# Layer 0 of a two-layer transformer kernel: two groups of transposes moved to a later stretch, and a PSUM copy with another priority

## The chip, the cores and the metric

The kernel runs on one core of one Trainium2 chip. The metric is the device time of one execution in microseconds; the kernel before takes 1139.03 us (median of 3 runs, 1138.77 to 1139.43).

TensorE (PE in the profile, PEld for its weight loads) multiplies matrices into PSUM. VectorE (DVE), ScalarE (ACT) and GpSimd (POOL) do the elementwise work, and SyncE (SP) issues most of the DMAs. Each engine runs its own instructions in order, and engines wait for each other by semaphores.

## What is computed

The input `x` is 4 sequences of 512 tokens with 256 features, all in float32. Four blocks follow each other, each added to its input after a layer norm without weights:

```
x = x + L0_attn(layernorm(x))   # 16 heads of 16, causal softmax, output projection w_out
x = x + L0_ffn(layernorm(x))    # per output feature: 8 router logits, the softmax's top 2
                                # weigh 8 expert outputs (expert_w); 2048 logits a token
x = x + L1_attn(layernorm(x))   # reads the array as (token, sequence): softmax over 4
                                # sequences, 16 query heads on 4 key heads of 128
x = x + L1_ffn(layernorm(x))    # gated MLP, 4-bit weights, 2048 inner features
```

The change touches the first block and the hand-over to the second.

## The kernel before

The tokens stay in SBUF (`xres`) as 16 groups of 128 tokens, in 4 blocks `j` of 4 groups; a block is a quarter of the causal order, for all 4 sequences.

**Layer 0 attention** runs over 44 batches `n`. A batch is a block of queries `j`, a sequence `s`, and 4, 2, 1 or 1 groups of 4 heads (for `j` = 0 to 3), so there are 4 batches in block 0, 8 in block 1 and 16 each in blocks 2 and 3. For each batch, `greatest` and `mask` make scores (L687, L700) whose maxima VectorE takes (L706); `shift` sends the maxima by DMA into an extra row of the queries. `powers` makes the scores again, transposed and shifted (L738), ScalarE takes the exponentials (L747), and GpSimd zeroes the masked triangle (L757). `mixed` multiplies them with the values (L774), and ScalarE copies the result out of PSUM (`avs`, L782). The score tiles share 5 PSUM banks (`ps_sc`), of which each of `greatest` and `powers` takes 4.

When the last heads of one `(j, s)` are mixed, `divided(j, s)` takes over. It transposes `avs` on TensorE (`av_T`, L792), divides by the sums on VectorE (`rden`, `oq`, L799 and L800), transposes the result back (`oq_T`, L809), and ScalarE copies it into `aT` (L812). After the fourth sequence, `aT` is multiplied with `w_out` (`o0`, L821) and added to `xres` (L831). Then `hidden_pieces(j)` normalises the new tokens (`norm_pieces`) and transposes them (`xT_ps`, L225) for the second block.

**Layer 0 FFN** is filler. `logit_pieces` and `result_pieces` each emit 64 products of 512 columns (`lg`, `eo`, both L249; 128 in all, each two matmuls), with VectorE work behind them (`weight_pieces`, `addition_pieces`) and ScalarE work (`lg` copies L312, `part` scalings L338, `spare` accumulations L430). What layer 0 leaves over goes on in layer 1 attention, where every `fill` gets a share of TensorE in proportion to the products left.

**Who orders the work.** The four compute engines run in the order in which the program emits, save for blocks under `tc.high_priority`. The order between the batches is planned by hand. Side work is written as generators (`Stream`) that yield `need(engine, cost, gap, cond)` before each step; `fill(PE=..., DVE=...)` opens one slot, counts `slot` up by one, and lets the streams go on while the budget of the engine that they ask for lasts. `gap` is the number of slots to pass after the stream's last step; `cond` must hold. The main loop does this for each batch:

```
with tc.high_priority(offset=AHEAD):      # AHEAD = 400
    greatest(n + 1); mask(n + 1); shift(n + 1)
fill(PE=..., DVE=2.6)                     # first stretch, an odd slot
with tc.high_priority(offset=AHEAD):
    mixed(n - 1); powers(n)
streams.insert(0, Stream(divided(...)))   # after the last heads of (j, s)
fill(PE=..., DVE=2.6)                     # second stretch, an even slot
```

`defer` puts ScalarE's accumulations off to the next slot. Those deferred in an odd slot come at the end of the next one, those deferred in an even slot at the start of the next one.

All side work that goes to PSUM shares the two banks of the pool `ps_dn`: `av_T`, `oq_T`, `xT_ps`, `lg`, `eo` and `o0`. A bank is free again when the engine that reads it is done.

When all 32 additions of the FFN are made, in head pass 10 of layer 1's 16, its weights' memory is given to the last block, and VectorE starts on the 4-bit weights (`dequant_pieces`).

Of the kernel before, what the change touches and what calls it, by code (L numbers as in the profile page):

```python
# [18 lines left out]
NS, NB = 4, 512  # L19
NT = 16  # L20
NC = 4
NBLK = 4
# [10 lines left out]
def tile_transformer(  # L33
# [18 lines left out]
    nc = tc.nc  # L52
# [56 lines left out]
    slot = 0  # L109

    def need(engine, cost, gap=0, cond=None):
        return engine, cost, gap, cond
# [54 lines left out]
    def norm_pieces(j, pool, small, out, deinterleave=False, cond=None):  # L167

        yield need("DVE", 1.0, cond=lambda: not normed and (cond is None or cond()))
        normed.append(j)  # L170
        st = small.tile([P, 4, 6], F32, tag="ln_st", name=f"ln_st{j}")
        mv = small.tile([P, 4, 2], F32, tag="ln_mv", name=f"ln_mv{j}")
        rs = small.tile([P, 4], F32, tag="ln_rs", name=f"ln_rs{j}")
        for t in range(4):
            if t == 2:
                yield need("DVE", 1.0)
            nc.vector.bn_stats(st[:, t, :], xres[:, 4 * j + t, :])
            nc.vector.bn_aggr(mv[:, t, :], st[:, t, :])
        yield need("DVE", 0.2)
        v = small.tile([P, 4], F32, tag="rs_v", name=f"rs_v{j}")  # L180
        nc.vector.tensor_scalar(v, mv[:, :, 1], EPS, None, ALU.add)  # L181
        nc.gpsimd.tensor_tensor(rs, v, minus_half, ALU.pow)  # L182
        xn = pool.tile([P, 4, HID], F32, tag="xn", name=f"xn{j}")
        for t in range(4):
            if t % 2 == 0:
                yield need("DVE", 0.9, not t)
            src, dst = xres[:, 4 * j + t, :], xn[:, t, :]
            if deinterleave:
                src = src.rearrange("p (k two) -> p two k", two=2)
                dst = dst.rearrange("p (two k) -> p two k", two=2)  # L190
            nc.vector.tensor_scalar(
                dst, src, mv[:, t, 0:1], rs[:, t : t + 1], ALU.subtract, ALU.mult
            )
        out.append(xn)
# [26 lines left out]
    def transposed(xn, hc, ps_pool, tag, name):  # L221

        ps = ps_pool.tile([P, 4, P], F32, tag=tag, name=name)
        for t in range(4):
            nc.tensor.transpose(ps[:, t, :], xn[:, t, hc * P : (hc + 1) * P], ident)  # L225
        return ps
# [52 lines left out]
    def hidden_pieces(b):  # L279

        out = []
        done = (4 * b - 5, 1)
        last = b == NBLK - 1
        yield from norm_pieces(b, b1, b2, out, cond=lambda: b < 2 or done in halves)
        xT = b2.tile([P, 2, 512], F32, tag="xT", name=f"xT{b}")
        for hc in range(2):
            yield need("PE", 0.5, 0 if hc else 1 + last)
            ps = transposed(out[0], hc, ps_dn, "dn", f"xT_ps{b}_{hc}")
            ps = ps.rearrange("p t q -> p (t q)")
            if hc:  # L290
                nc.scalar.activation(xT[:, hc, :], ps, AF.Identity, bias=last_16)
            else:
                nc.scalar.copy(xT[:, hc, :], ps)
        normed.clear()
        xTs[b] = xT
# [168 lines left out]
    with ExitStack() as l0:  # L464
# [202 lines left out]
        AHEAD = 400  # L667
# [116 lines left out]
        aTs = {}  # L784

        def divided(j, s):

            yield need("PE", 0.5, 1)
            avs = avs_of.pop((j, s))
            ps = ps_dn.tile([P, NH0, 32], F32, tag="dn", name=f"av_T{j}_{s}")  # L790
            for g in range(4):
                nc.tensor.transpose(  # L792
                    ps[:, 4 * g : 4 * g + 4].rearrange("p h d -> p (h d)"), avs[:, g], ident
                )

            rden = a2.tile([P, NH0], F32, tag="rden", name=f"rden_{j}_{s}")
            oq = a1.tile([P, NH0, 16], F32, tag="oq", name=f"oq_{j}_{s}")
            left["DVE"] -= 0.7
            nc.vector.reciprocal(rden, ps[:, :, 16])  # L799
            nc.vector.tensor_tensor(  # L800
                oq, ps[:, :, 0:16], rden.unsqueeze(2).to_broadcast([P, NH0, 16]), ALU.mult
            )

            yield need("PE", 0.3, 1, cond=lambda: slot % 2)
            if not s:
                aTs[j] = a1.tile([P, 2, 16, NS, 8], F32, tag="aT", name=f"aT{j}")
            ps = ps_dn.tile([P, 2, P], F32, tag="dn", name=f"oq_T{j}_{s}")
            for k in range(2):
                nc.tensor.transpose(  # L809
                    ps[:, k], oq[:, 8 * k : 8 * k + 8].rearrange("p h d -> p (h d)"), ident  # L810
                )
            nc.scalar.copy(aTs[j][:, :, :, s, :], ps.rearrange("p k (g b) -> p k g b", b=8))  # L812
            if s < NS - 1:
                return

            for t in (0, 2):
                yield need("PE", 1.75, 1 if j or not t else 0)
                ps = ps_dn.tile([P, 2, HID], F32, tag="dn", name=f"o0_{j}_{t}")
                for i in range(2):
                    for k in range(2):  # L820
                        nc.tensor.matmul(  # L821
                            ps[:, i],
                            lhsT=aTs[j][:, k, 4 * (t + i) : 4 * (t + i) + 4].rearrange(
                                "p g s b -> p (g s b)"
                            ),
                            rhs=wo[:, k, :], start=k == 0, stop=k == 1,
                        )
                if j:
                    yield need("DVE", 0.7, 1)
                both = xres[:, 4 * j + t : 4 * j + t + 2, :]  # L830
                nc.vector.tensor_tensor(both, both, ps, ALU.add)  # L831
            fold_at = streams.index(fold) if fold in streams else len(streams) - 5
            streams.insert(fold_at if j else 0, Stream(hidden_pieces(j)))


        ps = ps_mm.tile([P, 4, P], F32, tag="mm", name="idle")
        for i in range(5):
            nc.tensor.matmul(
                ps, lhsT=ident, rhs=ident.unsqueeze(1).to_broadcast([P, 4, P]),
# [46 lines left out]
        for n in range(NBT):  # L886
            j, s, gs = batches[n]
# [20 lines left out]
            if n and batches[n - 1][2][-1] == 3:  # L908
                streams.insert(0, Stream(divided(*batches[n - 1][:2])))
# [13 lines left out]
        mixed(NBT - 1)  # L923
        streams.insert(0, Stream(norm_pieces(0, b1, b2, normed_first)))
        last = Stream(divided(*batches[NBT - 1][:2]))
        streams.insert(0, last)
        while last.next is not None:
# [49 lines left out]
    with ExitStack() as l1:  # L977
# [249 lines left out]
        for p in range(-1, NP):  # L1227
            j, kv = divmod(p, NKV)
# [59 lines left out]
    with ExitStack() as f1:  # L1288
# [186 lines left out]
        f, k = firsts  # L1475
# [3 lines left out]
        for i in range(NBLK * NJ):  # L1479
            j, jj = divmod(i, NJ)  # L1480
# [12 lines left out]
            e, g = eg[:, 0], eg[:, 1]  # L1493
# [147 lines left out]
```

## Time and profile before

| | |
|---|---|
| median of 3 runs | 1139.03 us |
| profiled execution, own time | 1140.53 us |
| profiled execution, span | 1138.8 us |
| granted TensorE clock, mean | 0.999 |
| busy PE, PEld | 1109.8 us, 711.7 us |
| busy DVE, ACT, POOL | 842.3 us, 509.5 us, 247.2 us |
| `oq_T` L809, matmuls | 32, 6.3 us |
| `xT_ps` L225, matmuls | 64, 11.6 us (layer 0's and layer 1's) |
| `aT` L812, copies | 16, 5.9 us |

Layer 0 attention ends and layer 1 begins at about 385 us of the span, and the last block begins at about 820 us. The profile is one execution, and its span leaves out what lies before the first and after the last instruction. Ends of matmuls are modelled, so a busy TensorE can contain waits; they are seen in the distance from one block's start to the next.

### The profile page before, as it was taken

How to read it: one execution, taken by the hardware profiler on the slowest of the kernel's cores; microseconds unless marked ns; L12 is line 12 of the kernel's file. 1: busy time of each engine (PE TensorE's matmuls, PEld its weight loads, DVE VectorE, ACT ScalarE, POOL GpSimd, SP SyncE). 2: the span in 40 equal slices, each digit the busy share in tenths (PEclk: the TensorE clock that was granted, in tenths of full speed). 3: DMA queues.
4: the chain of work that ended last, by engine and by line, in shares of the span. 5: the costliest groups of instructions: out<-in, count | busy, mean ns of one | idle time of the engine just before them, and what ended most of it. 6: DMA issues, size and time to landing. Idle time of an engine off the chain costs nothing.

```text
span 1138.8 us, 19760 instructions
## 1 busy us (share of the span) xinstructions
PE 1109.8 (97%) x7430; PEld 711.7 (62%) x7430; DVE 842.3 (74%) x1856; ACT 509.5 (45%) x1190; POOL 247.2 (22%) x319
## 2 busy tenths in 40 slices
PE   9999999999999999999999999999999999999998
PEld 5666555555555445555555556556787788888885
DVE  6675988999999962867873695577479877778665
ACT  1445545665556543444444353243324444444442
POOL 8322222221111000000000000000064444353433
PEclk9999999999999999999999999999999999999999
DMA  4450010000000500000000002242002002002000
GB/s 133 110 134 5 17 25 2 2 1 3 2 2 2 184 2 1 1 1 1 1 1 1 1 2 37 66 110 68 18 1 54 22 19 75 1 19 75 18 2 19
DMA packets 32287, 35.13 MB, mean 31 GB/s; under 512 B 6024, under 2 KB 23176, under 8 KB 32192
## 3 DMA queue, kind: packets, MB, share of 16 engines
q1 hardware_dynamic: 31376, 32.69, 11.0%
q10 hardware_dynamic: 816, 1.18, 0.4%
q8 instruction: 59, 0.97, 0.3%
q14 instruction: 36, 0.29, 0.1%
HBM read 23.17 MB, written 6.29 MB: 26 GB/s over the span
## 4 chain that ended last, share of the span: by engine, by line
PE 67%; DVE 23%; ACT 4%; issue 3%; POOL 1%; DMA 1%; SPq 1%; DVEq 0%; POOLq 0%; ACTq 0%
PE qk_ps L1037 10%; PE lg_ps L249 8%; PE o L1128 8%; PE eg L963 7%; PE eo L249 7%; PE gu_first L963 5%; DVE mx L706 3%; PE yx L1344 3%; PE s L738 3%; PE s L687 3%; PE av L774 2%; PE yy L1344 2%; DVE it L1420 2%; DVE th L1419 2%; PE qk_ps L555 2%
## 5 line engine op out<-in xcount | busy, mean ns | idle before, releaser
L1037 PE MATMUL qk_ps<-xT,wqkv 128*128 128x512 f32 x320 | 148.7, 599 | 3.5 <-ACT v L1023 1.7
L249 PE MATMUL lg_ps<-rw,xT 128*128 128x512 f32 x256 | 122.5, 601 | 1.6 <-ACT aT L812 0.4
L249 PE MATMUL eo<-ew,xT 128*128 128x512 f32 x256 | 121.5, 600 | 1.1 <-ACT lg L312 0.5
L706 DVE TENSOR_REDUCE mx<-s 128x1 f32<-128x384 f32 (+3 forms) x176 | 100.5, 633 | 26.8 <-PE s L700 26.8
L1128 PE MATMUL o<-wpj,oT 128*128 128x256 f32 x512 | 119.1, 382 | 0.0
L757 POOL TENSOR_SCALAR_AFFINE_SELECT pt<-pt 128x256 f32<-128x256 f32 (+2 forms) x88 | 62.5, 715 | 243.3 <-ACT pt L747 242.5
L1128 PEld LDWEIGHTS o<-wpj,oT 128*128 128x128 f32 x512 | 96.0, 190 | 27.0 <-issue 13.5
L1037 PEld LDWEIGHTS qk_ps<-xT,wqkv 128*128 128x128 f32 x320 | 59.1, 190 | 73.2 <-issue 58.4
L747 ACT ACTIVATE pt<-s 128x512 f32<-128x512 f32 (+1 forms) x176 | 84.0, 563 | 37.6 <-PE s L738 37.6
L182 POOL TENSOR_TENSOR ln_rs<-rs_v,minus_half 128x4 f32<-128x4 f32 x12 | 13.6, 1135 | 366.0 <-DVE rs_v L181 366.0
L338 ACT ACTIVATE part<-eo,c 128x256 f32<-128x256 f32 x128 | 53.6, 472 | 84.0 <-PE eo L249 72.7
L1531 ACT COPY gu_first<-eg 128x512 f32<-128x512 f32 x28 | 16.0, 570 | 134.2 <-PE eg L963 129.9
L249 PEld LDWEIGHTS eo<-ew,xT 128*128 128x128 f32 x256 | 46.2, 190 | 46.3 <-issue 38.5
L249 PEld LDWEIGHTS lg_ps<-rw,xT 128*128 128x128 f32 x256 | 46.1, 190 | 46.3 <-issue 37.5
L1322 POOL TENSOR_TENSOR it<-it 128x512 f32<-128x512 f32 x30 | 38.2, 1273 | 146.6 <-PE gu_first L963 66.9
L312 ACT COPY lg<-lg_ps 128x512 f32<-128x512 f32 x64 | 37.6, 588 | 71.8 <-PE lg_ps L249 71.8
L1041 ACT COPY qT<-qk_ps 128x512 f32<-128x512 f32 x64 | 37.5, 586 | 64.7 <-PE qk_ps L1037 64.7
L1344 PE MATMUL yx<-it,wd 128*128 128x256 f32 x240 | 66.2, 379 | 0.0
L738 PE MATMUL s<-qk 32*128 32x128 f32 x1280 | 56.6, 287 | 0.7
L687 PE MATMUL s<-qk 32*128 32x128 f32 (+3 forms) x512 | 56.7, 465 | 0.4
L438 DVE SCALAR_TENSOR_TENSOR junk<-lg,w 128x256 bf16<-128x256 f32 x128 | 54.9, 429 | 0.0
L365 DVE TENSOR_TENSOR part<-part 128x512 f32<-128x512 f32 x32 | 22.4, 700 | 43.9 <-ACT part L338 43.9
(305 smaller groups left out, 2202.5 us busy)
## 6 DMA issues: line engine op xcount, KB each, us to landing
qk<-stage SPq DMA_DIRECT2D x56, 64.0 KB
wqkv<-in_w_qkv SPq DMA_DIRECT2D x8, 320.0 KB
rw<-in_router_w SPq DMA_DIRECT2D x8, 256.0 KB
ew<-in_expert_w SPq DMA_DIRECT2D x8, 256.0 KB
qk<-mT SPq DMA_DIRECT2D x128, 0.5 KB
wpj<-in_w_proj SPq DMA_DIRECT2D x1, 2048.0 KB
dq_sgu<-in_gate_up_s SPq DMA_DIRECT2D x64, 32.0 KB
xres<-in_x SPq DMA_DIRECT2D x3, 512.0 KB
```

Of the source, the lines that this page charges most:

```text
L249: nc.tensor.matmul(ps, lhsT=xT[:, hc, (g % 4) * P : (g % 4 + 1) * P], rhs=w[:, hc, 2 * pair : 2 * pair + 2, :].rearrange("p e o -> p (e o) ...
L338: nc.scalar.mul(part[:, e % 4], ps[:, i], c[:, e : e + 1])
L438: stt(junk, d[:, e], 0.0, w1, ALU.is_gt, ALU.mult, accum_out=c1[:, e : e + 1])
L687: nc.tensor.matmul(tiles[h][:, b * nk : (b + 1) * nk].rearrange("p (c k) -> p c k", k=P), lhsT=queries(j, g)[r, s], rhs=qk[r, g, : j + 1, ...
L706: nc.vector.tensor_reduce(maxes[:, :nb, h], ps[:, : nb * nk].rearrange("p (b k) -> p b k", b=nb), AX.X, ALU.max,)
L738: nc.tensor.matmul(tiles[h][:, at : at + P], lhsT=qk[r, g, c, s, :], rhs=queries(j, g)[r, s], start=True, stop=True,)
L747: nc.scalar.activation(pt[:, i, : nb * nk], tiles[2 * pair + i][:, : nb * nk], AF.Exp, scale=0.25)
L757: nc.gpsimd.affine_select(out=last, in_=last, compare_op=ALU.is_ge, fill=0.0, base=0, pattern=pattern, channel_multiplier=-1,)
L963: nc.tensor.matmul(ps[:, w], lhsT=lhs(w), rhs=rhs, start=start and not i and not w, stop=i == len(terms) - 1 and w == 1, skip_group_check= ...
L1037: nc.tensor.matmul(ps, lhsT=wqkv[:, hc, kv, h, :], rhs=xT[:, hc, :], start=hc == 0, stop=hc == 1,)
L1128: nc.tensor.matmul(ys[t // 2][:, t % 2], lhsT=state["o"][:, h, t * P : (t + 1) * P], rhs=wpj[:, HPK * kv + h, :], start=kv == 0 and h == 0 ...
L1344: nc.tensor.matmul(ps, lhsT=lhs(jj), rhs=its[8 * j + jj][:, plane], start=start and not n, stop=n == 1, skip_group_check=not start,)
```

## The change

The step that transposes the divided output (`oq_T`) waited for an odd slot, the first stretch; it now waits for an even one, the second stretch, except for the last batch (block 3, sequence 3), where any slot will do. The transposes of normalised tokens in `hidden_pieces` were asked for one slot after the norm's last step, in the last block two; now it is two in every block. The copy of `oq_T` into `aT` is emitted under the same high priority as the batches' own work.

```diff
@@ hidden_pieces
         done = (4 * b - 5, 1)
-        last = b == NBLK - 1
         yield from norm_pieces(b, b1, b2, out, cond=lambda: b < 2 or done in halves)
         xT = b2.tile([P, 2, 512], F32, tag="xT", name=f"xT{b}")
         for hc in range(2):
-            yield need("PE", 0.5, 0 if hc else 1 + last)
+            yield need("PE", 0.5, 0 if hc else 2)
@@ divided
+            last_batch = j == NBLK - 1 and s == NS - 1
             yield need("PE", 0.5, 1)
...
-            yield need("PE", 0.3, 1, cond=lambda: slot % 2)
+            yield need("PE", 0.3, 1, cond=lambda: last_batch or not slot % 2)
...
-            nc.scalar.copy(aTs[j][:, :, :, s, :], ps.rearrange("p k (g b) -> p k g b", b=8))
+            with tc.high_priority(offset=AHEAD):
+                nc.scalar.copy(aTs[j][:, :, :, s, :], ps.rearrange("p k (g b) -> p k g b", b=8))
```

## The prediction

> **What bounds the kernel now.** I read the page's busy shares and slices first, then the busy times by stage, then TensorE's timeline through layer 0.
>
> ```profile
> PE 1109.8 (97%) x7430; PEld 711.7 (62%) x7430; DVE 842.3 (74%) x1856; ACT 509.5 (45%) x1190; POOL 247.2 (22%) x319
> ...
> DVE  6675988999999962867873695577479877778665
> ```
>
> TensorE is the bound of the whole span. In slices 6 to 14, which are layer 0's late batches, VectorE is nearly as full. The same by stage (us, then busy us of PE, PEld, DVE, ACT, POOL, granted clock, DMA share, GB/s):
>
> ```profile
> 150.00:395.00 245.00, 238.51 (x2360) 127.63 (x2359) 228.01 (x548) 140.29 (x382) 43.66 (x63) 0.99 0.06 19
> 395.00:700.00 305.00, 301.64 (x1442) 165.95 (x1441) 200.26 (x514) 135.31 (x351) 3.34 (x3) 1.00 0.02 6
> 166.00:171.00 5.00, 4.80 (x58) 3.40 (x58) 4.93 (x13) 1.91 (x4) 0.14 (x1) 0.66 0.01 3
> ```
>
> From 150 to 395 us VectorE is busy 228.0 of 245 us and TensorE 238.5: two engines at their limit. In layer 1 (second row) VectorE has 105 us to spare and TensorE 3. PE's busy time contains waits inside its blocks, so stalls must be read from the starts of blocks. TensorE's timeline (start us, us, block, idle and releaser):
>
> ```profile
> 165.17 0.40 PE L700 MATMUL s<-later,ident_h 128*128 128x128 bf16 x4
> 166.20 0.44 PE L809 MATMUL oq_T<-ident,oq 128*128 128x128 f32 x2 [0.63 <-DVE oq L800]
> 166.61 2.21 PE L225 MATMUL xT_ps<-ident,xn 128*128 128x128 f32 x8
> 168.75 1.51 PE L774 MATMUL av<-pt,va 128*32 128x128 f32 x24
> ...
> 182.51 0.86 PE L774 MATMUL av<-pt,va 128*32 128x128 f32 x24
> ...
> 195.14 0.40 PE L700 MATMUL s<-later,ident_h 128*128 128x128 bf16 x4
> 196.58 0.41 PE L809 MATMUL oq_T<-ident,oq 128*128 128x128 f32 x2 [1.04 <-DVE oq L800]
> ```
>
> Each transpose asked for in the first stretch waits for VectorE's division, which is queued behind filler work. At 166 us three such waits meet, the clock drops to half for about 3 us (0.66 in the row 166:171), and the next block takes 1.51 us where its like takes 0.86. Last, ScalarE's queue in front of the last transposed copy, and the output product that waits for it:
>
> ```profile
> 373.29 0.42 ACT L430 ACTIVATE spare<-owing__4754 128x256 bf16<-128x256 f32 x1 [2.95 <-DVE owing__4754 L423]
> ...
> 373.70 0.35 ACT L812 COPY aT<-oq_T 128x256 f32<-128x256 f32 x1
> ...
> 374.11 1.99 PE L821 MATMUL o<-wo,aT 128*128 128x256 f32 x8 [1.73 <-ACT aT L812]
> ```
>
> The copy had its input at about 369.9 us, but stood behind an accumulation that waited 2.95 us for VectorE.
>
> **The change, part by part.** No instruction is added or removed; every term is a shift in the engines' order. I call the fill after the maxima of batch n stretch nA and the one after its powers nB.
>
> 1. The transposes of the divided output go from A to B. With normal spacing from mask to next block of 0.23 us, the mask at 165.17 is followed after 1.03, the one at 195.14 after 1.44, and the one at 224.35 after 0.53 (224.88). Excess 0.79 + 1.21 + 0.29 = 2.3 us. In B they stand behind the mixed values and the powers, 1.8 us later; the division is done by then. Gain 2.3 us.
>
> 2. Transposes of normalised tokens, one slot later for blocks 0 to 2. Eight took 2.49 us from 88.28 to the next block at 90.77, and 2.14 us from 166.61 to 168.75; at about 0.11 us each they need 0.88. Of the excess of 1.6 + 1.25 us, I leave some 0.5 for ScalarE's copy, which the logits need at once in either order. Gain 2.3 us, and the 0.65 us of the half-clock block (1.51 against 0.86).
>
> 3. The copy on ScalarE. In the built order it stands straight behind the four exponentials of its batch in all 15 ordinary cases, and in the last case ahead of the accumulations that blocked it. It stands in the same places with the priority taken out, since the accumulations of a B stretch are put out at its end anyway: the word "priority" buys nothing by itself, and the move to B does. Gain: TensorE's idle 1.73 us at 374.11 and 0.40 us before logits at about 286. Holding a dn bank until the exponentials end (four of 0.56 us) is covered by the one product of 1.75 us that follows.
>
> 4. The last batch. Its transposes now stand straight behind those of its mixed output, with no product between (before: one, 1.72 us). They wait for reciprocal and product, 0.24 + 0.42 us and two hand-overs: a loss of about 1.0 us.
>
> 5. Filler thins out. Counting products (two matmuls of 512 columns, 4 x 0.43 = 1.72 us) by stretch in the built orders, layer 0 holds 63 before and 59 after; all 128 are done by head pass 11 of layer 1 in both, and TensorE's order is the same from pass 12. Four products, 6.9 us, leave layer 0 and return in layer 1: no net cost if TensorE is the bound in both. But they leave uneven stretches. Without a product (or nearly) are 19A, 41A and 42A before; 07A, 17A, 18A, 20A, 22A, 26A, 29A, 39A and 40A after. What an empty stretch costs, TensorE shows:
>
> ```profile
> 214.24 0.95 PE L738 MATMUL s<-qk 32*128 32x128 f32 x24
> 215.01 2.47 PE L687 MATMUL s<-qk 32*128 32x384 f32 x8
> ...
> 339.99 2.85 PE L738 MATMUL s<-qk 32*128 32x128 f32 x32
> ...
> 347.70 1.95 PE L738 MATMUL s<-qk 32*128 32x128 f32 x32
> ```
>
> An empty A lengthens the powers behind it: 1.95 us where 1.17 is normal (0.8), and in block 2 1.50 for 0.95 (0.55). That is 2.15 us before (0.55 + 2 x 0.8) and 5 x 0.55 + 4 x 0.8 = 5.95 after. An empty B lets the next scores wait for the exponentials: 2.47 for 0.93, 1.54 us; with only the first transposes in it, 0.75 to 1.16. Stretches 06B, 16B, 19B, 23B, 27B and 36B make 7.2 us before; 06B, 20B, 24B, 28B, 35B and the missing product of 43B (about 1.9) make 6.5 after. Loss 3.8 - 0.7 = 3.1 us.
>
> Sum: 2.3 + 2.3 + 0.65 + 2.1 = 7.35 gained, 1.0 + 3.1 lost: about -3.2 us, taken as -3.0. Bounds of the unknown: an empty A may cost nothing, where VectorE would have made TensorE wait anyway, or as much as the worst late-maxima row (2.85 us, 1.68 over normal). I take the middle since the rows at 183 and 348 us are empty A's themselves.
>
> 6. Layer 1: the division of labour moves some 40 VectorE instructions there, into its 105 us of room. The dequantisation ends one step later; its last product (1.23 us) then falls behind the last softmax instead of ahead of it, into an 8 us wait of VectorE for the residual. SP's transposing loads for the last stage come after the third weight load, some 80 us before use. GpSimd's roots move with the norms; it is 22% busy. Zero.
>
> The profile's span is 1138.8 us and its own time 1140.53, 1.5 us above the median of 1139.03. With -3.0 the span would be 1135.8, the profile's time 1137.5, and the median 1136.0.
>
> A rule against the change: the Trainium skill, "TensorE: Matmul & The Clock Gate", section "HAM oscillation", asks that TensorE have no idle gap over about 3.4 us, or its clock halves. The row 166:171 halved with no idle of more than 0.63 us between blocks, so the measurement is stricter than the page. By the page the thinned stretches cost nothing; by the row, one more thin spell (06B with 07A, or 16B to 18A) could cost the same 0.65 us or a little more.
>
> **The rivals.** (a) VectorE sets the pace of layer 0. For: 93% busy there, and 4.9 us less of its work, by instruction means, stands before the last maxima. Then TensorE's saved waits are absorbed: -4.9 to the last maxima, -1.7 for the product missing in the tail, -1.7 + 1.0 for items 3 and 4 there, +6.9 in layer 1: -0.4 us, 1138.6. Against: TensorE's own blocks of a full batch (7.2 us) also fill the period.
>
> (b) Slower: the powers behind the empty A's wait for late maxima. Six more such stretches at 1.68 us instead of 0.55 to 0.8 cost 10.1 us in place of 3.8, and -3.0 becomes +3.3: 1142.3. It decides from about 1.1 us for each empty A. For: two batches' filler is now asked for in one B, and VectorE's segment before the maxima of batch 20, 23, 28 and 37 sums to 8.1 to 8.8 us. Against: equally long segments stand before, at other batches.
>
> (c) The priority reorders nothing: already in item 3, no change to the sum.
>
> **How the numbers follow.** Forecast (-3.0, between -2.4 and -6.0) 0.46; (a) 0.24; (b) 0.30. About 0.2%, 2.3 us, is what a measurement of this kernel can tell from no change, so these are the chances of faster, same and slower. The range runs from 1133.0, the forecast with most of the 3.8 us of empty A's free, to 1143.0, a little beyond (b).
>
> **What would show it.** Right: oq_T without idle before it except once at the end; o<-wo,aT without wait for the copy; clock 1.00 around 160 to 180 us; layer 1 starting some 8 to 10 us sooner and taking some 7 us longer. Wrong: powers (L738) of 2 us and more at 17, 20, 22, 26 and 39; a second half-clock spell; or a layer 1 that stalls where the late products fall.

## The result: slower, and outside the predicted range

| | before | after |
|---|---|---|
| median | 1139.23 us (4 runs) | 1154.82 us (4 runs, 1153.45 to 1154.91) |
| ratio | | 1.0127 [1.0112, 1.0142] |
| profiled execution: span, own time | 1138.8, 1140.53 us | 1153.1, 1154.79 us |
| layer 1's first head pass | 393.5 us | 400.7 us |
| last block's first product | 815.6 us | 830.0 us |

Forecast was 1136.0 us, with a range of 1133 to 1143. Layer 0 became 7.2 us longer, where some 8 to 10 us less were expected. Layer 1 became 7.2 us longer (429.3 against 422.1), close to the predicted 6.9 (but see point 6). The last block is unchanged (323.1 against 323.2). Some executions of single kernels ran at a much lower granted clock; they are left out of every ratio, and the profiles of e4 and e11, which show such executions, are not compared.

The page of the changed kernel, its busy shares and VectorE's 40 slices:

```profile
PE 1117.1 (97%) x7430; PEld 717.6 (62%) x7430; DVE 841.7 (73%) x1856; ACT 508.5 (44%) x1190; POOL 243.3 (21%) x319
...
DVE  7666758999999756676974485677568877778665
```

The same instructions, and TensorE "busy" 7.3 us longer: its blocks hold more waiting inside. VectorE has a hole in slices 5 and 6 (7 and 5 tenths), where it was at 9 and 8 before. By stage (us, then busy us of PE, PEld, DVE, ACT, POOL, granted clock, DMA share, GB/s), the changed kernel:

```profile
150.00:395.00 245.00, 234.55 (x2392) 128.25 (x2391) 218.53 (x525) 134.46 (x368) 39.06 (x63) 0.99 0.04 11
400.70:830.00 429.30, 424.41 (x2174) 241.92 (x2172) 285.43 (x685) 184.79 (x436) 6.43 (x5) 1.00 0.10 24
150.00:200.00 50.00, 46.12 (x449) 25.86 (x447) 34.73 (x87) 22.15 (x61) 7.50 (x13) 0.93 0.08 12
```

and the last stretch in the kernel before:

```profile
150.00:200.00 50.00, 47.98 (x480) 26.17 (x481) 46.34 (x112) 26.39 (x73) 11.77 (x15) 0.97 0.04 7
```

Between 150 and 200 us both engines that were at their limit are idle for longer, VectorE by 11.6 us. I measured each block of TensorE from its start to the next one's and took off the usual distance of its kind. What is left between 30 and 400 us is 25.8 us before and 40.9 after, 15.1 more. By releaser, the powers' wait for VectorE's maxima goes from 7.7 to 16.2 us (a batch's powers need score banks that the maxima of the next batch still hold; I call this wait late maxima); the rest are waits that hardly stood in the profile before. TensorE's timeline of the changed kernel shows all kinds (start us, us, block, idle and releaser):

```profile
61.25 0.38 PE L809 MATMUL oq_T<-ident,oq 128*128 128x128 f32 x2
62.30 1.12 PE L554 MATMUL qk_ps<-xT,wp 128*128 128x512 f32 x2 [0.66 <-DVE oq L800]
...
96.01 0.60 PE L225 MATMUL xT_ps<-ident,xn 128*128 128x128 f32 x4
98.08 0.66 PE L225 MATMUL xT_ps<-ident,xn 128*128 128x128 f32 x4 [1.47 <-ACT aT L813]
...
152.58 3.70 PE L249 MATMUL eo<-ew,xT 128*128 128x512 f32 x8
...
157.07 0.40 PE L699 MATMUL s<-later,ident_h 128*128 128x128 bf16 x4
160.16 3.48 PE L822 MATMUL o<-wo,aT 128*128 128x256 f32 x8 [2.69 <-ACT part L337]
...
176.08 2.40 PE L737 MATMUL s<-qk 32*128 32x128 f32 x24
178.41 0.44 PE L809 MATMUL oq_T<-ident,oq 128*128 128x128 f32 x2
178.69 0.60 PE L225 MATMUL xT_ps<-ident,xn 128*128 128x128 f32 x4
180.33 1.11 PE L225 MATMUL xT_ps<-ident,xn 128*128 128x128 f32 x4 [1.04 <-ACT aT L813]
...
349.05 2.26 PE L737 MATMUL s<-qk 32*128 32x128 f32 x32
351.23 0.66 PE L792 MATMUL av_T<-ident,avs 128*128 128x128 f32 x4
```

- **Late maxima.** The powers of batch 17 take 2.33 us (176.08 to 178.41) where 24 such matmuls take 0.88; those of batch 40 2.18 where 32 take 1.10. Behind the nine empty stretches A that the prediction named the excess is 1.88, 1.45, 0.67, 1.80, 1.59, 0.67, 1.03, 0.85 and 1.08 (07 to 40): 11.0 us.
- **Held banks.** At 98.08 and 180.33 xT_ps waits for the copy aT, which stands behind four exponentials. At 62.30 (and twice more in block 0) the projections wait for the division, since av_T and oq_T stand in one stretch and hold both dn banks.
- **A staging transfer.** Two products `eo0_0` and `eo0_1` stand in one stretch (152.58, 8 matmuls). Their scaling on ScalarE waits 4.90 us:

```profile
159.27 1.57 ACT L337 ACTIVATE part<-eo,c 128x256 f32<-128x256 f32 x4 [4.90 <-DMA qk<-stage]
```

The tile `part` reuses the buffer of `stage3_1`, whose DMAs still read it. Before the change the two products stood in different stretches, and a wait of 3.77 us at this place let one bank free, so that TensorE did not stop for it. Now both dn banks are held, o0_1_2 waits 2.69 us for one, until 160.16.

- **Half-clock spells.** Within that last wait, at 159.8 us, TensorE's clock falls to half for 3.4 us, and so it does at 180.3 us (within the second wait of xT_ps) and at 439.7 us, in layer 1. The profile before has one such spell, at 167.0 us. A spell costs at most half its length, so the two more are worth up to 3.4 us (an estimate from the rows).

```profile
159.80:163.20 3.40, 3.04 (x7) 2.50 (x8) 1.54 (x3) 1.03 (x3) 0.00 (x0) 0.50 0.01 1
180.30:183.60 3.30, 3.27 (x7) 1.92 (x8) 1.70 (x3) 1.15 (x2) 1.22 (x2) 0.50 0.00 0
439.70:443.10 3.40, 3.40 (x5) 1.35 (x4) 3.37 (x16) 0.57 (x1) 0.00 (x0) 0.50 0.00 0
```

### The profile page after: what moved, and what is told of

It reads as the page before. It is cut to its first block, busy times and chain, and to the rows that moved or that the text cites. A ratio compares the mean times of both kernels' runs of the same rounds, so it can differ in the third digit from the quotient of the medians.

```text
span 1153.1 us, 19741 instructions
## 1 busy us (share of the span) xinstructions
PE 1117.1 (97%) x7430; PEld 717.6 (62%) x7430; DVE 841.7 (73%) x1856; ACT 508.5 (44%) x1190; POOL 243.3 (21%) x319
## 4 chain that ended last, share of the span: by engine, by line
PE 71%; DVE 21%; ACT 3%; issue 2%; POOL 1%; DMA 1%; SPq 1%; DVEq 0%; POOLq 0%; ACTq 0%
PE qk_ps L1038 10%; PE o L1129 8%; PE eo L249 8%; PE lg_ps L249 8%; PE eg L964 7%; PE gu_first L964 5%; PE s L737 3%; PE yx L1345 3%; PE s L686 3%; DVE mx L705 3%; PE v_ps L1020 2%; PE av L773 2%; PE yy L1345 2%; DVE it L1421 2%; DVE th L1420 2%
## 5 line engine op out<-in xcount | busy, mean ns | idle before, releaser
L756 POOL TENSOR_SCALAR_AFFINE_SELECT pt<-pt 128x256 f32<-128x256 f32 (+2 forms) x88 | 58.5, 670 | 259.8 <-ACT pt L746 259.7
L737 PE MATMUL s<-qk 32*128 32x128 f32 x1280 | 62.0, 287 | 2.3 <-DVE mx L705 1.2
L737 PEld LDWEIGHTS s<-qk 32*128 32x128 f32 x1280 | 48.5, 185 | 16.6 <-issue 8.5
```

Source lines behind the costliest of these rows:

```text
L737: nc.tensor.matmul(tiles[h][:, at : at + P], lhsT=qk[r, g, c, s, :], rhs=queries(j, g)[r, s], start=True, stop=True,)
L756: nc.gpsimd.affine_select(out=last, in_=last, compare_op=ALU.is_ge, fill=0.0, base=0, pattern=pattern, channel_multiplier=-1,)
```

## The experiments

Theory T: the two moves together make the filler uneven, and waits of several kinds, late maxima above all, come up behind it. Rivals: the PSUM bank held behind the exponentials, the later tokens, the staging transfer. Medians of "before" differ between sets (1139.2 to 1140.6 us), so runs are compared by ratio; the last column is (ratio - 1) x 1139.

| | edit | ratio [95%] | us |
|---|---|---|---|
| | the change | 1.0127 [1.0112, 1.0142] | +14.5 |
| e1 | oq_T to B, priority | 1.0002 [0.9992, 1.0011] | +0.2 |
| e2 | later tokens only | 0.9969 [0.9959, 0.9979] | -3.5 |
| e6 | the change, block 0's tokens as before | 0.9999 [0.9990, 1.0009] | -0.1 |
| e8 | later tokens in blocks 1 and 2, priority | 1.0000 [0.9991, 1.0010] | 0.0 |
| e3 | the change, oq_T in another pool | 1.0104 [1.0079, 1.0130] | +11.8 |
| e4 | the change, staging tile elsewhere | 1.0093 [1.0076, 1.0110] | +10.6 |
| e9 | e3 and e4 | 1.0061 [1.0038, 1.0084] | +6.9 |
| e10 | the change, one product a stretch | 1.0041 [1.0026, 1.0055] | +4.7 |
| e13 | e10 and e3 | 1.0037 [1.0025, 1.0050] | +4.2 |
| e5 | the change, oq_T booked at 0.0 | 1.0035 [1.0024, 1.0045] | +4.0 |
| e14 | the change, oq_T booked at 0.5 | 1.0071 [1.0053, 1.0088] | +8.1 |
| e7 | before, six stretches A emptied | 1.0114 [1.0094, 1.0134] | +13.0 |
| e11 | e2 and priority | 0.9954 [0.9941, 0.9967] | -5.2 |
| e12 | e11 and larger budgets | 1.0007 [0.9996, 1.0019] | +0.8 |

### Each move alone: e1, e2, e6, e8

```diff
 e1, against the change
-            yield need("PE", 0.5, 0 if hc else 2)
+            yield need("PE", 0.5, 0 if hc else 1 + last)
 e2, against before
-            yield need("PE", 0.5, 0 if hc else 1 + last)
+            yield need("PE", 0.5, 0 if hc else 2)
 e6, against the change
-            yield need("PE", 0.5, 0 if hc else 2)
+            yield need("PE", 0.5, 0 if hc else (1, 2, 2, 2)[b])
 e8, against before (and the copy under high priority)
-            yield need("PE", 0.5, 0 if hc else 1 + last)
+            yield need("PE", 0.5, 0 if hc else (1, 2, 2, 2)[b])
```

e1: 

> Only the transposes of the divided output move to the second stretch, with the copy's priority; the normalised tokens' transposes stay where they were before. In the built order layer 0 then holds as many filler products as before (before 59 in the stretches between batches, changed kernel 56), and six stretches A that the changed kernel leaves empty (07, 17, 18, 20, 22, 26) are filled. Theory T (the loss comes from the thinned stretches, which only the two moves together make, and from the wait of the part scaling at 155 us): close to before, 1137 to 1141 us, powers late by under 10 us in all where the changed kernel has 16. Rival B (the move to B itself costs, since the PSUM bank of oq_T is held behind the exponentials): 1147 us or more, with waits of xT_ps, o and lg for the copy aT. Rival G (the gap of two slots costs): before minus 2 to 3, 1136.

e2: 

> Only the transposes of normalised tokens move one slot later; the transposes of the divided output stay in the first stretch and the copy keeps its old priority. Layer 0 again holds 59 products, with 33A and 41A newly or still empty and 17A, 19A, 42A filled. Theory T: 1136 to 1140 us, a little below before, for the waits of xT_ps for the normalised tokens (1.2 us) and the half-clock block are gone. Rival B: the same. Rival G (a later start of the logits is what costs): 1147 us or more.

e6: 

> The changed kernel with the tokens' transposes of block 0 alone asked for one slot later instead of two; blocks 1 and 2 keep two. In the built order this alone brings back 59 products and fills 07A, 14A, 17A, 18A, 20A, 22A, 26A, 29A, 39A and 40A. Theory T': the whole loss hangs on block 0's first transposes being a slot later in a kernel whose oq_T is in B, which delays the first logits and thins every stretch behind: 1138 to 1141 us, VectorE busy 46 us or more of the 50 from 150 us on (changed kernel 34.7). Rival: the later slots of blocks 1 and 2 carry part of it: 1145 to 1150 us.

e8: 

> The kernel before, with the tokens' transposes of blocks 1 and 2 alone one slot later and the copy's priority; oq_T stays in the first stretch. The two waits of xT_ps for the normalised tokens and the half-clock spell go (3 us in the prediction's rows, less the 1 to 1.5 us of logits that then wait for the copy xT), and the last copy no longer stands behind an accumulation (up to 1.7 us): 1135 to 1138 us. Rival (the gain of the kernel with only the later slots, 3.5 us, came from block 0): 1139.

Neither move costs anything alone: the first changes nothing (+0.2), the second gains 3.5 us. Together they lose 14.5. And the loss hangs on one slot: with block 0's transposes back in their old slot (e6) the changed kernel is as fast as before. In its stage row VectorE's hole is gone and the clock is full; e6:

```profile
150.00:200.00 50.00, 48.38 (x529) 26.28 (x531) 47.74 (x114) 28.31 (x77) 9.17 (x15) 1.00 0.07 11
```

The block around 96 us shows the slot. In e6 block 0's tokens are transposed in 07A, ahead of the powers, and oq_T stands alone with a product behind them; in the changed kernel all of it stood in 07B, behind powers that had no cover, in the banks that oq_T held. e6:

```profile
94.45 1.98 PE L249 MATMUL lg_ps<-rw,xT 128*128 128x512 f32 x4 [0.24 <-ACT xT L292]
96.36 1.08 PE L773 MATMUL av<-pt,va 128*32 128x128 f32 x32
97.37 1.17 PE L737 MATMUL s<-qk 32*128 32x128 f32 x32
98.47 0.44 PE L809 MATMUL oq_T<-ident,oq 128*128 128x128 f32 x2
98.75 1.88 PE L249 MATMUL lg_ps<-rw,xT 128*128 128x512 f32 x4
```

e8 answered a side question: the later slots of blocks 1 and 2, which carried most of the prediction's 2.3 + 0.65 us, gain nothing. Nor did the priority: the last output product still waits 1.74 us for the copy in e8's timeline (before: 1.73). So most of what e2 gains must come from block 0's slot too, which with oq_T in A fills 17A, 19A and 42A. In e2's profile layer 1 is shorter (418.6 us for the same 63 products, before 422.1) and layer 0 longer; but this is the slowest of e2's nine executions (1138.86 us, the fastest 1134.82), so where the gain lies is not settled.

### The waits one by one: e3, e4, e9

```diff
 e3, against the change
-            ps = ps_dn.tile([P, 2, P], F32, tag="dn", name=f"oq_T{j}_{s}")
+            ps = ps_mm.tile([P, 4, P], F32, tag="mm", name=f"oq_T{j}_{s}")[:, :2]
 e4, against the change
-                        [P, 2, 512], F32, tag="hi4" if j == 2 else "part", name=f"stage{j}_1"
+                        [P, 2, 512], F32, tag="hi4" if j == 2 else "xn", name=f"stage{j}_1"
```

e3: 

> The changed kernel with the PSUM tile of oq_T in the pool of the projections instead of the two dn banks; the order of all engines is that of the changed kernel. Theory T: the waits for the copy aT in front of xT_ps (1.5 us) and of block 0's projections for the division (1.5 + 0.8 us) go, the late powers stay at about 16 us: 1151 to 1153 us. Rival B (banks held behind the exponentials are the main cost): 1144 us or less. If the projections' own pool becomes the wait instead: 1154 to 1156.

e4: 

> The changed kernel with the last staging tile of the positions' columns (stage3_1) in the buffers of the normalised tokens instead of those of part, so that the first scaling part0_0 does not wait for the staging DMAs; the order of the compute engines is that of the changed kernel. Theory T counts 3 to 5 us for this wait (4.9 us of ScalarE at 159 us, o0_1_2 2.7 us late, the half-clock block after it): 1149 to 1152 us, and a clock of 1.00 from 150 to 200 us. Rival T' (late maxima behind thin stretches alone): 1154 us, the next wait takes its place within two batches. Rival S (the staging wait is the whole of it): 1145 us or less.

e9: 

> The changed kernel with both of the earlier edits: oq_T in the projections' PSUM pool, and the last staging tile in the buffers of the normalised tokens; the order of the compute engines stays that of the changed kernel. One at a time they gave 4.5 and 3.4 us. If they are separate waits the sum is 8 us: 1147 us, with the late powers still at 16 us in the trace: then the other 7 us are the thin stretches' (theory T). If one wait takes the other's place: 1149 to 1151. If the two are all of the loss: 1141 or less.

By ratio e3 gives back 2.7 us, e4 3.9, both together 7.6. (The expectation of e9 has larger figures for each, taken from medians of two sets.) The interval of e3 overlaps that of the change, so its 2.7 us alone is not clear of noise; e4 and e9 are. The figures fit two separate waits that are together about half of the loss (by the interval of e9, some 5 to 10 us). The late maxima are untouched by either: 16.6 us in e3 and 15.3 in e9, the changed kernel 16.2.

### The spread of the filler: e10, e5, e14, e13

```diff
 e10, against the change: products (lg and eo) wait for the next stretch if this one has one
+                    room() and g // 4 in xTs and (0, pair) in folded ...
+                    and room() and h in weights and weights[h][1] < slot ...
 e5 (0.0) and e14 (0.5), against the change
-            yield need("PE", 0.3, 1, cond=lambda: last_batch or not slot % 2)
+            yield need("PE", 0.0, 1, cond=lambda: last_batch or not slot % 2)
```

e10: 

> The changed kernel with one more condition: no stretch of layer 0's batches takes a second filler product. Both moves stay, block 0's late chain too, and layer 0 keeps the changed kernel's 56 products; only their spread is evener: from batch 16 on the stretches A without a product are 16, 29, 35, 39 instead of 17, 18, 20, 22, 26, 29, 39, 40. Theory T (a price for each empty stretch A, about 1.2 us in the changed kernel and 2 us in the kernel made for it): 1147 to 1150 us. Rival (the late chain itself costs, wherever the products stand): 1153 to 1156.

e5: 

> The changed kernel with one number changed: the step that emits oq_T is booked at 0.0 of the slot's TensorE budget instead of 0.3. Both moves and the priority stay, but layer 0 gets its 59 products back and the empty stretches A from batch 16 on go from 17, 18, 20, 22, 26, 29, 39, 40 to 17, 18, 33, 42; with it block 0 is as before the change up to batch 12. Theory T (uneven filler and late maxima behind it): 1138 to 1143 us, late powers of 8 to 11 us. Rival H (both moves together delay the FFN's chain, whatever the filler does): 1150 us or more.

e14: 

> The changed kernel with oq_T booked at 0.5 instead of 0.3. In layer 0 three products fewer than the changed kernel (53); from batch 16 on the empty first stretches are 25, 27, 38, 39, 41 (changed kernel: eight), the empty second ones 16, 17, 18, 20, 24, 28, 29, 35, 40 (changed kernel: 20, 24, 28, 35, 43). If only empty first stretches cost: 1147 to 1149 us. If empty second ones cost as well, 1 to 1.5 us each as the scores wait for the exponentials: 1151 to 1156 us, with the waits of scores for exponentials at 10 us or more in place of 6.

e13: 

> The changed kernel with at most one filler product in a stretch of layer 0 and with oq_T in the projections' PSUM pool. Alone they gave 9.2 and 4.5 us. If the two causes are separate the sum is 13 to 14 us: 1140 to 1142 us, which with the staging wait (gone with the spread) is the whole loss. If they share their gain: 1143 to 1145 us, and a third cause is open.

Both moves stay in all four, and block 0's tokens are late in all. e10 spreads the products and gives back 9.8 us, more than expected: late maxima fall to 12.4 us, scores waiting for exponentials from 6.2 to 3.9, and the staging wait no longer reaches TensorE, since the two `eo` stand apart. e5 gives back 10.5 us by another way, one number of the booking (1143.91 us, just above its range). So the spread is the main cause, and not a late chain in itself.

The built order shows how the number acts. In block 2 a stretch B has 2.2: 2.2 - 0.3 - 1.85 leaves 0.05, and what is above zero lets a second product in; the account is then at -1.80, and the next A's 1.8 leaves nothing. 21B and 25B hold oq_T and two products, 22A and 26A are empty. Booked at 0.0, 0.3 us is left for the A, which gets its product.

e14 landed where T's first branch put it (1147.44 us), but nearly with the second branch's sign: scores wait 9.6 us for exponentials instead of 6.2, and late maxima still take 13.3. An empty B is paid for as well, here with 3.4 us of such waits.

e13 did not add up: 0.5 us beyond e10, where 2.7 was to be had by e3, itself not clear of noise. The bank's waits are gone in its trace, but logits now wait for the copy xT, and the clock is at half from 96.1 us on, before that wait begins, e13:

```profile
96.12 1.91 PE L225 MATMUL xT_ps<-ident,xn 128*128 128x128 f32 x8
98.66 3.78 PE L249 MATMUL lg_ps<-rw,xT 128*128 128x512 f32 x4 [0.63 <-ACT xT L299]
...
96.10:102.90 6.80, 6.17 (x18) 3.22 (x20) 1.65 (x7) 3.51 (x8) 2.81 (x4) 0.50 0.00 1
```

This profile is of an execution of 1148.85 us, where the other five took 1143.6 to 1144.3, so it does not show why the median gained so little.

What stays of the loss in e10 is in the stage row of its layer 1:

```profile
391.30:818.90 427.60, 422.69 (x2173) 241.31 (x2171) 285.52 (x685) 185.06 (x436) 6.44 (x5) 1.00 0.10 24
```

By the built order 61 products stand ahead of layer 1 (before: 65), so layer 1 takes 427.6 us instead of 422.1. Layer 0 ends only 2.2 us sooner for the four products that it lost (6.9 us).

### The price of an empty stretch A: e7

```diff
 e7, against before
-            fill(PE=(2.0, 2.0, 1.8, 1.6)[j], DVE=2.6)
+            moved = 1.8 if n in (20, 24, 28, 34, 37, 40) else 0.0
+            fill(PE=(2.0, 2.0, 1.8, 1.6)[j] - moved, DVE=2.6)
...
-            fill(PE=(2.4, 2.4, 2.2, 2.0)[j], DVE=2.6)
+            fill(PE=(2.4, 2.4, 2.2, 2.0)[j] + moved, DVE=2.6)
```

> The kernel before, with the product of six first stretches (20, 24, 28, 34, 37, 40) put into the second stretch of the same batch; nothing else moves and layer 0 keeps 59 products. This is the price of an empty stretch A by itself. The prediction's 0.55 us (block 2) and 0.8 us (block 3) make 3 x 0.55 + 3 x 0.8 = 4.1 us: 1143. The price that the changed kernel showed (1.2 us on average) makes 7.3 us: 1146; 1.68 us each makes 10 us: 1149. Rival (the product is missing in the next scores as well as in these powers, or VectorE's pace hides it): no change, 1139.

13.0 us for six: 2.2 us each with what the clock adds, against the predicted 0.55 to 0.8, above even the worst case given (1.68). Two of them in TensorE's timeline, e7:

```profile
187.26 0.48 PE L738 MATMUL s<-qk 32*128 32x128 f32 x2
188.65 2.57 PE L738 MATMUL s<-qk 32*128 32x128 f32 x22 [0.91 <-DVE mx L706]
191.15 1.11 PE L792 MATMUL av_T<-ident,avs 128*128 128x128 f32 x4
192.06 5.49 PE L249 MATMUL eo<-ew,xT 128*128 128x512 f32 x8
...
348.96 3.27 PE L738 MATMUL s<-qk 32*128 32x128 f32 x30 [1.71 <-DVE mx L706]
352.16 1.12 PE L792 MATMUL av_T<-ident,avs 128*128 128x128 f32 x4
353.06 3.49 PE L249 MATMUL eo<-ew,xT 128*128 128x512 f32 x4
```

The powers of batch 20 take 3.89 us (187.26 to 191.15) for 0.88. While they run, at 189.0 us, the clock falls to half, and it stays there for 6.8 us: the two products behind them take 5.42 us (192.06 to 197.48), where the changed kernel's pair at 152.58 takes 3.63. The stretch rows, e7:

```profile
185.60:189.00 3.40, 2.18 (x32) 1.36 (x29) 3.33 (x6) 0.27 (x1) 1.26 (x1) 1.00 0.00 0
189.10:195.80 6.70, 6.70 (x30) 4.35 (x30) 6.46 (x15) 1.72 (x5) 0.91 (x2) 0.50 0.00 0
253.90:257.30 3.40, 3.40 (x32) 2.66 (x25) 3.26 (x8) 2.06 (x4) 0.54 (x2) 0.50 0.01 1
349.50:356.20 6.70, 6.64 (x36) 4.53 (x37) 5.62 (x21) 2.06 (x4) 0.92 (x2) 0.50 0.00 0
```

At half clock TensorE counts as busy nearly throughout. Late maxima in all are 16.4 us, 8.8 more than before; with 13.0 us lost, some 4 us are the clock and the rest. Part of the 8.8 is the clock too, since the spells begin inside late powers: 17.1 us of this profile ran at half against 3.4 before, worth up to 6.8 us (an estimate). A product moved by one stretch, with the same work in the batch, costs more than the product itself (1.72 us). As e7 fills a B for each A that it empties, this is the price of the two together.

### A better version: e11, e12

```diff
 e11: e2, and the copy of oq_T under tc.high_priority(offset=AHEAD)
 e12: e11, and
-            yield need("PE", 0.3, 1, cond=lambda: slot % 2)
+            yield need("PE", 0.5, 1, cond=lambda: slot % 2)
-            fill(PE=(2.0, 2.0, 1.8, 1.6)[j], DVE=2.6)
+            fill(PE=(2.0, 2.0, 2.0, 1.8)[j], DVE=2.6)
```

e11: 

> The kernel with the later tokens' transposes alone (1136.9 us), with the copy's priority added; oq_T stays in the first stretch. The last copy aT then stands ahead of the accumulations: the 0.9 us for which the output product waited for it go. 1135.5 to 1136.9 us. Rival (the copy is ready late anyway): no change.

e12: 

> The kernel with the later tokens' transposes and the copy's priority, and the filler's budgets set so that fewer first stretches stay empty: oq_T booked at 0.5, first stretches of blocks 2 and 3 with 2.0 and 1.8 instead of 1.8 and 1.6. Empty A from batch 7 on: 07, 33, 43 (without the budgets 07, 13, 33, 41, 43); layer 0 takes three products more, layer 1 three fewer. Theory T (late powers fall with the number of empty A's, at 1 to 2 us each): 1132 to 1135 us. Rival (VectorE paces these batches, so more TensorE filler does not help it): 1136 to 1138 us.

e11 is the fastest: 1135.98 us, 0.46% below before. But on every engine it has e2's built order, instruction by instruction, so it is a second measurement of e2 rather than a gain over it (0.9954 and 0.9969, the intervals overlap), and its expectation, which let the priority move the copy, was wrong. e12 lost all of the gain. Its late maxima fell as T said, from 8.6 (e2) to 5.9 us, but scores then waited 10.2 us for the exponentials instead of 7.6, as products left B for A: e12

```profile
339.75 0.40 PE L700 MATMUL s<-later,ident_h 128*128 128x128 bf16 x4
339.98 1.51 PE L249 MATMUL eo<-ew,xT 128*128 128x512 f32 x3
```

(the scores in front of 339.75 came 1.86 us late). Counting empty A's alone was too simple.

## Why the prediction was wrong, point by point

1. **oq_T from A to B: the trace shows the gain, and a wait that was not seen.** oq_T's own waits are gone but for the last batch. In block 0, "the division is done by then" failed: av_T and oq_T stand in one stretch, and the next filler waits for the division, three times 0.77 us. Alone, with the priority, this move gains nothing (e1: +0.2 us), where items 1, 3 and 4 sum to a gain of 3.4: the waits that it saves come back elsewhere, as rival (a) said of TensorE's waits; which waits, no run shows.
2. **Tokens a slot later: wrong.** The waits of xT_ps for the norm are gone (1.2 us before, 0 after), but instead of the half-clock spell at 167 us there are two, at 160 and 180 us, and a third in layer 1: the prediction's own sign of being wrong. (The spell before began at 167.0 us, 0.4 us into the eight transposes at 166.61, so up to 0.9 of the 1.25 us counted there as waiting was the clock, by estimate.) e8 shows that the slots of blocks 1 and 2 gain nothing, and e6 that block 0's slot, costed like the others, decides the whole case.
3. **ScalarE's copy.** Right at the end: o<-wo,aT has no idle before it any more.

```profile
384.01 1.98 PE L249 MATMUL eo<-ew,xT 128*128 128x512 f32 x4 [0.93 <-ACT part L337]
385.83 1.89 PE L822 MATMUL o<-wo,aT 128*128 128x256 f32 x8
```

"Holding a dn bank until the exponentials end is covered by the one product" failed: at 98.08 and 180.33 no product stood there, but the second xT_ps, which needs a bank. With point 1's block-0 waits this is the 2.7 us that e3 gave back (not clear of noise). That the word "priority" reorders nothing (rival c) holds in all three pairs: the change, before and e2 keep their built orders with it and without it. What let the last copy through is that the last batch may take any slot.

4. **The last batch: right.** Predicted 1.0 us, measured 1.07 us, of which the row shows 0.81 as idle:

```profile
377.48 0.44 PE L809 MATMUL oq_T<-ident,oq 128*128 128x128 f32 x2 [0.81 <-DVE oq L800]
```

5. **The filler: the step that failed.** The list of empty stretches was right, their price was not: 11.0 us measured in the nine named, for 5.95. The three named of the kernel before (19, 41, 42) measure 2.3 us, for 2.15, so the loss in this term is 8.7 us in place of 3.8. That is rival (b)'s mechanism, above its deciding point (1.22 us each against 1.1), and the rows that it took its price from are too cheap by e7. Late maxima at stretches that were not empty (12, 19, 27, 36: 5.2 us), which the forecast left out, add nothing: before, at other batches, they are about 5.4 us (7.7 less 2.3). Two costs were put at nothing: the two more half-clock spells (up to 3.4 us, of which the prediction weighed one, at 0.65) and the staging transfer (3.9 us by e4), which no rival held, since the prediction looked at how many products a stretch had and not at which two: `eo0_0` and `eo0_1` in one stretch take both banks while their reader waits.
6. **Four products moved: half right.** Layer 1 is 7.2 us longer, near the 6.9 forecast, but in part by luck: one half-clock spell (up to 1.7 us) lies in it, and in e10, with the same four products there and no spell, it is 5.5 us longer. And "no net cost" needs layer 0 to give them back, and it did not: in e10, with the spread mended, layer 0 is shorter by 2.2 us of 6.9. Rival (a), which had layer 0 shorten with the VectorE work that leaves it (4.9 us up to the last maxima), does not show in e10 either.

The clock rule that was weighed: the Trainium skill, "TensorE: Matmul & The Clock Gate", section "HAM oscillation", has the clock halve behind idle gaps over about 3.4 us. The measurement decides here: in e7 the clock halved at 189.0 us with no shown idle over 0.91 us, TensorE being shown busy for 2.18 of the 3.40 us before. Nor does the shown idle decide it: in the kernel before, around the wait of 1.73 us at 374.11, TensorE is busy for 1.67 of 3.40 us, and the clock stays full:

```profile
371.80:375.20 3.40, 1.67 (x7) 0.99 (x6) 3.33 (x13) 1.51 (x5) 0.74 (x1) 1.00 0.00 0
375.20:378.60 3.40, 3.29 (x11) 1.64 (x10) 2.68 (x11) 0.74 (x3) 0.00 (x0) 1.00 0.00 0
```

The same page's section "A second HAM failure mode: psum-queue depth-cycling" is nearer: there short idle times between groups of matmuls, repeated in every turn through the PSUM banks, are enough. The powers of e7 wait bank by bank for the maxima, which would fit; no run here counts those waits one by one.

**What stays open.** The parts overlap (e9 gives back 7.6 us, e10 9.8, the whole is 14.5), so no clean split is possible; the share of the clock in them is not separated either. About 4 us are left in e5, e10 and e13. In e10 the products that layer 0 lost would fill this; e5 has all of them back, and its rest (late maxima 11.7 us, scores 8.2) lies in the empty stretches that it still has.

## What to carry to other kernels

Where filler hides a wait between two batches, price a moved step by what it does to the filler's booking, and price an empty stretch by making one (e7), not from the cheapest rows at hand. Two moves that are harmless or good alone must be built together: here a leftover of 0.05 us in a slot's budget let a second product in and emptied the next stretch. And look at which tiles stand next to each other: two that share a small pool, with a reader that waits for something else, stop the bound engine.

## What was not expected of the hardware

An empty stretch is not only paid with its wait. Inside a powers block that took 3.89 us instead of 0.88 (with 0.91 us of it shown as idle), TensorE's granted clock fell to half for 6.8 us (0.50 in the row 189.10:195.80), and two products took 5.42 us instead of 3.63. What tips the clock is not shown: it fell in e7 with TensorE shown busy for 2.18 of the 3.40 us before, and stayed full in the kernel before with 1.67. That waits inside blocks, which the busy column counts as work, count for the clock is a guess that no run here tests.
